# A Gram block of 64 tokens by 133 split into two of 32 by 95, four side by side in the array's columns, and the blocks of the first image set apart from each other

## The chip, the cores and the metric

The kernel runs on one core of a Trainium2 chip. The metric is the device time of the program in microseconds. Three runs of the kernel before gave 2585.49, 2586.68 and 2586.95 us; their median, 2586.68 us, is the time before. The profile shown is of a further execution.

## The reference, cut to what matters

Eight images of 768 channels and 32 x 32 tokens go through two layers. The first is a group norm and an attention with 12 heads, whose scores come from the variances of keys and values, then a projection and the residual. The second layer is what the change is about:

```python
norm = jnp.sqrt(jnp.sum(feature * feature, axis=1, keepdims=True))
feat_n = feature / jnp.maximum(norm, EPS)
feat_pad = jnp.pad(feat_n, ((0, 0), (0, 0), (PAD, PAD), (PAD, PAD)))
corr = jnp.stack([jnp.sum(feat_pad[:, :, r:h + r, cc:w + cc] * feat_n, axis=1) for r, cc in _offsets()], axis=1)
x = jnp.concatenate([feature, corr], axis=1)
out = jnp.einsum('bchw,oc->bohw', x, conv_w) + conv_b[None, :, None, None]
```

`feature` is the group norm of the first layer's result. The 28 offsets lie within three rows and three columns of a token. So `corr` needs, for each token, dot products over the 768 channels with some of its neighbours.

## The kernel before, in words

**The Gram blocks.** By symmetry only neighbours in the same row and in the three rows below are computed. Each image is cut into 8 blocks of 4 rows by 32 columns (`t` from 0 to 7), and each block into a left and a right half of 16 columns. `Corr.gram(t)` (from L1140) computes the products of each half's 64 tokens with a window of 7 rows by 19 columns, 133 tokens, around it; the last block has only 4 rows below its top, so 76 tokens. The 64 tokens are the stationary operand and the window is the moving one. The two halves stand side by side in the array's columns: the left half writes partitions 0 to 63 of the PSUM tile `gr`, the right half 64 to 127. There are 6 chunks of 128 channels, so a gram has 12 matmuls in the program. All is fp32, and the hardware runs each fp32 matmul as two, so the trace has 24 per gram.

**Around it.** `Corr.turn(t)` (L1138) puts the stationary tokens of block t into one contiguous tile `turn`: two instructions, one per half. They run on POOL for images 0 to 6, where `turnpool` has one buffer, so block t+1 is turned when gram t has read the tile; for the last image they run on ACT, into buffers of the pool `expool`. After the matmuls, `out` copies the PSUM tile to one of the tiles `win` (by DVE; by ACT for the last image), of which two alternate for t from 0 to 6, and SyncE stores it to DRAM (`windowed`, L1171): two DMAs of 64 rows. After the grams 3 and 7 the diagonals are read back (`dd`, L1185), scaled with the inverse norms (`rn` by POOL at L1201, `dn` by DVE), transposed by TensorE (`ct`, L353), stored (L1222), gathered (L1233 to L1239) and multiplied to `cs`, the 28 correlation channels. The matmuls of L1059, L1272 and L1370 add them to the convolution. They have 28 rows of the array by 128 columns.

**Other widths of matmul.** Nearly all other matmuls go in halves of 64 columns too: `halves` (L350) for keys, values, projection and convolution, and L800 for the attention's products (`av`). `ones_products` (L831, tile `den`) is the one place that uses four groups of 32 columns: four matmuls of 32 x 512 in the program, eight in the trace.

**What sets the order.** The order on every engine is fixed when the program is built. A planner (`Clock`) holds a time of its own; every unit of TensorE work has a planned duration (`KV_US` 1.93, `T_US` 2.58, `STEP_US` 1.73, `GRAM_US` 1.4), and jobs for other engines are put in at planned times (`later.after`). In the loop over b, image b's attention runs next to the second layer of image b-1. `work_off` alternates: an attention run of four steps (16 matmuls `av` in the program) when its exponentials are planned to be there, otherwise the next unit of `rest`. The grams of image b-1 lie in the list `beside`; `next_to` takes the first of them. It is called before and after every attention run, and from places inserted in `rest` (at 3 and 7; in the turn b = 1, which has the first image's grams, at 7, 11 and 15). `remaining` takes what is left near the end of `rest`. The last image's eight grams stand in `rest` in a row, after two units.

**Who reads what.** In `rest` at (d = 1, n = 0) a unit also emits `make_sums` (L636 to L642), eight POOL instructions for the tile `s`. POOL does them in the order in which they are emitted, among the turns.

Of the kernel before, what the change touches and what calls it, by code (L numbers as in the profile page):

```python
# [13 lines left out]
P = 128  # L14
NB, C, H, W = 8, 768, 32, 32
N = H * W
J = C // P
NH, HD = 12, 64
HP = NH // 2
MT = N // P  # L20
# [7 lines left out]
RUNS = ((0, 0, 4), (31, -1, 3), (62, -2, 5), (93, -3, 7))  # L28
HW = W // 2
TALL, WIDE = MT // 2 + 3, HW + 3  # L30
AHEAD_OF = [o for first, _, count in RUNS for o in range(first, first + count)][1:]
NA = len(AHEAD_OF)
PAD = 99
SPAN = TALL * WIDE
WIN = SPAN + 3
PITCH = WIN + 3
# [17 lines left out]
TAIL = 0.0  # L54
EXP, SUM, STEP_US = 1.07, 1.15, 1.73
KV_US, T_US, CORR_US = 1.93, 2.58, 1.2
GRAM_US = 1.4
WARM, BRIDGE = 42, (3, 7)


# [13 lines left out]
FOUR = P // 4  # L74
# [12 lines left out]
def windows(ap, *dims):  # L87

    return bass.AP(tensor=ap.tensor, offset=ap.offset, ap=[list(d) for d in dims])


class Clock:


    def __init__(self):
        self.now, self.count, self.jobs = 0.0, 0, []
        self.act, self.rows, self.poll = 0.0, ([], []), lambda: None
        self.dve = 0.0

    def after(self, us, job):  # L100
        self.count += 1
# [71 lines left out]
def two_layers(ctx, tc, x, wkv, wproj, bproj, wconv, wcorr, bconv, out):  # L173
# [28 lines left out]
    clock = Clock()  # L202
    later = clock
    vector = Vector(nc.vector, clock)
    ready = set()
# [4 lines left out]
    def other(shape, name):  # L210
        return smp.tile(shape, F32, tag="sm", name=name)
# [16 lines left out]
    def act_copy(us, to, at):  # L228
        nc.scalar.copy(to, at)  # L229
        clock.act = max(clock.act, clock.now) + us  # L230
# [172 lines left out]
    for j in range(J):  # L403
        for hf, queue in enumerate((nc.sync, nc.scalar)):
            at = slice(hf * HF, (hf + 1) * HF)
# [18 lines left out]
    for base, sign in ((0, 1), (3, -1)):  # L424
        nc.gpsimd.affine_select(
            out=group, in_=group, compare_op=ALU.is_ge, fill=0.0, base=base,
# [25 lines left out]
    windowed = [dconst.tile([MT, P * (PITCH + 2)], F32, name=f"windowed{i}") for i in range(2)]  # L452
# [668 lines left out]
    class Corr:  # L1121
# [18 lines left out]
        def gram(self, t):  # L1140

            b = self.b
            tall = min(TALL, H - 4 * t)
            n = tall * WIDE
            if t not in self.turned:
                self.turn(t)
            block = self.turned[t]
            ps = other([P, SPAN], f"gr{b}_{t}")
            for j in range(J):
                image = self.f[:, j, :].rearrange("p (y x) -> p y x", x=W)  # L1150
                for side in range(2):
                    left = side * (HW - 3)
                    nc.tensor.matmul(  # L1153
                        ps[side * HD : (side + 1) * HD, :n].rearrange("p (y x) -> p y x", x=WIDE),
                        lhsT=block[:, j, side, :],
                        rhs=image[:, 4 * t : 4 * t + tall, left : left + WIDE],
                        start=j == 0, stop=j == J - 1,
                    )
            for ahead in range(t + 1, min(t + (3 if b == NB - 1 else 2), MT)):
                if ahead not in self.turned:  # L1160
                    self.turn(ahead)

            def out():
                win = wins[t % 2 if t < MT - 1 else 2]
                if b < NB - 1:
                    vector.tensor_copy(win[:, :n], ps[:, :n])
                else:
                    act_copy(0.3, win[:, :n], ps[:, :n])
                for side in range(2):
                    to = windowed[b % 2][t : t + 1, side * (HD * PITCH + HD - 3) :]  # L1170
                    nc.sync.dma_start(  # L1171
                        out=windows(to, (HW * PITCH - 3, 4), (PITCH, HW), (1, WIN)), in_=win[side * HD : (side + 1) * HD, :]
                    )
                if t % 4 == 3:
                    later.after(4.0, lambda: self.diagonals(t // 4))

            later.after(GRAM_US + 0.25, out)

        def diagonals(self, hf):
# [48 lines left out]
        def gather(self):  # L1228
# [6 lines left out]
            for n, (first, apart) in enumerate(PICKED):  # L1235
                k, row = 3 * n, 2 + AHEAD_OF.index(first)
                nc.sync.dma_start(out=u[k : k + 3, :], in_=windows(r[row : row + 1, PAD:], (apart * ROW, 3), (1, N)))
# [15 lines left out]
    class Conv:  # L1253
# [24 lines left out]
        def low_residual(self):  # L1278
            self.early = True
            for n in range(JH):  # L1280
                later.after(1.5 * n, lambda n=n: self.residual(n))
# [106 lines left out]

    def remaining(beside):
        while beside:  # L1390
            next_to(beside)

    def next_to(beside):

        if beside and ready.issuperset(beside[0][1]):
            us, _, unit = beside.pop(0)
            unit()
            clock.pass_time(us)
# [94 lines left out]
    def next_image(b):  # L1493
        load_image(b)
        xn = images[b]
        clock.after(12.0, lambda: first_norm(b, xn, 1.2, lambda norm: norm.apply(xn, xn, ("xn", b), 1.2)))
# [34 lines left out]
    def fill_t(count):  # L1531
        for n in range(count):
            later.after(1.0 * n, t_stream.fill)

    def start_corr(b):
        corrs.append(Corr(b, layer1[b][0]))
        corrs[-1].turn(0)

    second, corrs = [], []
# [5 lines left out]
    for b in range(NB + 1):  # L1545
        rest, attention, ots, beside = [], None, None, []
        if b < NB:

            ots = [v.rearrange("p t r d -> p (t r d)") for v in kv.vt]
            rest += kv.units(1)  # L1550
            if b:
                rest.insert(len(rest) - 5, (0.0, (), lambda: conv.low_residual()))
            attention = Attention(b, kv, ots)
        if b:
            has_f = ("f", b - 1),
            if b > 1:
                clock.wait(*has_f, ready=ready)
            f, acc = layer1[b - 1] if b > 1 else first_f * 2
            corr = corrs.pop() if 1 < b < NB else Corr(b - 1, f) if b == NB else None
            conv = Conv(  # L1560
                b - 1, f, images[b] if b < NB else acc, (lambda b=b: next_image(b + 1)) if b + 1 < NB else lambda: None
            )
            if b < NB:

                def low_residual(b=b, f=f):
                    for n in range(JH):
                        later.after(1.5 * n, lambda n=n: nc.sync.dma_start(out=f[:, n, :], in_=xv[b, :, n, :]))

                conv.then = low_residual
            grams = [(GRAM_US if t < MT - 1 else 0.9, has_f if b > 1 else has_f + ("turned",), lambda t=t: (corr or corrs[0]).gram(t)) for t in range(MT)]  # L1570
            first, start = (0.0, has_f, conv.sums.first), (0.0, (), conv.start)
            if b < NB:
                beside = grams
                for n in (3, 7) if b > 1 else (7, 11, 15):
                    rest.insert(n, (0.0, has_f, lambda: next_to(beside)))
                rest.insert(len(rest) - 4, (0.0, has_f, lambda: remaining(beside)))
                rest.insert(len(rest) - 4, first)
                rest += [start] + conv.units()
                if b == NB - 1:
                    rest.insert(len(rest) - 3, (0.0, (), conv.set_aside))  # L1580
            else:
                units, parts = conv.units(), conv.corr_units()
                rest += [first, start] + units[:2] + grams + units[2:17]
                for n, unit in enumerate(units[17:]):
                    rest += parts[n : n + 1] + [unit]
        else:
            more = [(us, (("xn", 1),) * (n > 1), unit) for n, (us, _, unit) in enumerate(kv1.units(0))]
            rest.insert(len(rest) - 3, (0.0, (), lambda: apply_second(0)))
            rest += [(0.0, (), lambda: apply_second(1))] + more[:20] + [(0.0, (), lambda: fill_t(3))] + more[20:]
            rest += [(0.0, (), lambda: fill_t(TBLOCKS - 3))]  # L1590
        work_off(rest, attention, beside)
        assert not beside
        if b < NB:
            project(b, ots, conv.wide if b == NB - 1 else None)
            if b == 0:
                kv = kv1
                kv.place_values()
            elif b + 1 < NB:
                clock.wait(("xn", b + 1), ready=ready)
                kv = KeysValues(b + 1, images[b + 1])  # L1600
                units = kv.units(0)
                units.insert(len(units) - 6, (0.0, (("f", b),), lambda: start_corr(b)))
                work_off(units)
            else:
                clock.wait(("f", b), ready=ready)
# [36 lines left out]
```

## Time and profile before

| | |
|---|---|
| median of three runs | 2586.68 us |
| the profiled execution, its own time | 2586.23 us |
| its span, first to last instruction | 2584.4 us |
| TensorE matmuls `gr` of 64 x 133 and 64 x 76 in the trace | 1344 and 192 |
| TensorE's clock | 1.0 over the whole span |
| DMA | 448.18 MB, mean 173 GB/s |
| SyncE: stores of `windowed` | 128, each 503 to 711 ns of issue (median 518) |

Some words on reading. A matmul's duration in the trace includes the time until its last result is out, and matmuls overlap, so a stream is read from the distance of the starts. The view by groups gives the busy time of a group with overlaps counted once. In the timeline the columns are the start (us), the length (us), engine, line, operation, result and operands, rows x columns of the array, shape and number; in brackets stands the engine's idle time before it and what ended it. PEld is the loading of the stationary operand. Some matmul records can be missing.

### The profile page before, as it was taken

How to read it: one execution, taken by the hardware profiler on the slowest of the kernel's cores; microseconds unless marked ns; L12 is line 12 of the kernel's file. 1: busy time of each engine (PE TensorE's matmuls, PEld its weight loads, DVE VectorE, ACT ScalarE, POOL GpSimd, SP SyncE). 2: the span in 40 equal slices, each digit the busy share in tenths (PEclk: the TensorE clock that was granted, in tenths of full speed). 3: DMA queues.
4: the chain of work that ended last, by engine and by line, in shares of the span. 5: the costliest groups of instructions: out<-in, count | busy, mean ns of one | idle time of the engine just before them, and what ended most of it. 6: DMA issues, size and time to landing. Idle time of an engine off the chain costs nothing.

```text
span 2584.4 us, 40568 instructions
## 1 busy us (share of the span) xinstructions
PE 2577.0 (100%) x14798; PEld 1317.4 (51%) x14798; DVE 1614.2 (62%) x4117; ACT 1367.6 (53%) x1844; POOL 426.0 (16%) x449
## 2 busy tenths in 40 slices
PE   9999999999999999999999999999999999999999
PEld 5654364444764347643456434664347443575333
DVE  6868835775347853478534885358853578536874
ACT  1497179801697117970179701897018970199600
POOL 4320130004300043000430004300033001331000
PEclk9999999999999999999999999999999999999999
DMA  8866366355563655636556365563655636545333
GB/s 294 290 224 222 102 210 187 119 195 170 184 202 102 198 168 175 206 97 208 167 174 201 97 212 171 169 199 108 216 171 159 208 109 215 164 142 166 116 111 108
DMA packets 324718, 448.18 MB, mean 173 GB/s; under 512 B 59811, under 2 KB 245523, under 8 KB 324519
## 3 DMA queue, kind: packets, MB, share of 16 engines
q1 hardware_dynamic: 322454, 442.24, 53.6%
q10 hardware_dynamic: 2064, 3.34, 0.4%
q8 instruction: 118, 1.93, 0.3%
q14 instruction: 82, 0.66, 0.1%
HBM read 376.70 MB, written 64.40 MB: 171 GB/s over the span
## 4 chain that ended last, share of the span: by engine, by line
PE 98%; POOL 1%; DVE 0%; issue 0%; DMA 0%; ACT 0%; SPq 0%; POOLq 0%; ACTq 0%; DVEq 0%
PE x L350 35%; PE av L800 25%; PE y L350 18%; PE z L350 10%; PE own L350 5%; PE gr L1153 3%; PE den L831 1%; PE warm L419 1%; PE den L887 1%; POOL turn L1138 0%; PE y L1059 0%; PE z L1059 0%; PE cc L1272 0%; DVE acc L167 0%; DMA windowed<-win 0%
## 5 line engine op out<-in xcount | busy, mean ns | idle before, releaser
L774 ACT ACTIVATE ex<-bc,nk 128x1024 f32<-128x1024 f32 x768 | 827.3, 1137 | 414.3 <-DVE v L167 146.5
L800 PE MATMUL av<-ex,v 128*64 128x512 f32 x3072 | 692.1, 593 | 0.1
L800 PEld LDWEIGHTS av<-ex,v 128*64 128x64 f32 x3072 | 325.2, 137 | 323.0 <-issue 209.9
L784 ACT ACTIVATE junk<-bk,vm 128x1024 bf16<-128x1024 f32 x368 | 420.4, 1142 | 28.4 <-DMA bk<-kdr 18.8
L167 DVE TENSOR_TENSOR acc<-acc,ex 128x1024 f32<-128x1024 f32 x300 | 344.6, 1211 | 0.0
L229 ACT COPY kp<-x 128x384 f32<-128x384 f32 x28 | 13.3, 478 | 510.1 <-PE x L350 508.6
L350 PE MATMUL y<-kv,s 128*64 128x384 f32 x1488 | 265.7, 487 | 0.4 <-POOL s L636 0.4
L350 PE MATMUL x<-kv,xn 128*64 128x384 f32 x1512 | 259.9, 486 | 0.0
L350 PE MATMUL x<-kv,s 128*64 128x384 f32 x1488 | 257.3, 487 | 0.0
L350 PEld LDWEIGHTS x<-kv,xn 128*64 128x64 f32 x1512 | 136.6, 137 | 107.0 <-issue 85.9
L350 PEld LDWEIGHTS x<-kv,s 128*64 128x64 f32 x1488 | 140.0, 137 | 93.9 <-issue 72.7
L350 PEld LDWEIGHTS y<-kv,s 128*64 128x64 f32 x1488 | 134.3, 137 | 94.2 <-issue 76.0
L530 POOL TENSOR_TENSOR rstda<-vea,neghalf 128x1 f32<-128x1 f32 x8 | 4.8, 595 | 965.1 <-DVE vea L167 965.1
L1138 POOL TENSOR_TENSOR turn<-f,ones 128x384 f32<-128x384 f32 x112 | 110.9, 1010 | 242.7 <-PE gr L1153 167.9
L350 PE MATMUL z<-kv,xn 128*64 128x384 f32 x768 | 133.5, 486 | 0.0
L350 PE MATMUL x<-f,wt 128*64 128x512 f32 x504 | 118.3, 592 | 0.0
L167 DVE TENSOR_TENSOR v<-y,v 128x128 f32<-128x128 f32 x180 | 40.9, 282 | 117.9 <-PE y L350 117.9
L636 POOL TENSOR_TENSOR s<-xn 128x384 f32<-128x384 f32 x64 | 65.7, 1035 | 281.9 <-PE x L350 169.4
L167 DVE BATCH_NORM_STATS2 vbn<-v 128x6 f32<-128x64 f32 x720 | 101.5, 209 | 0.0
L350 PEld LDWEIGHTS z<-kv,xn 128*64 128x64 f32 x768 | 72.4, 137 | 49.8 <-issue 40.3
L1153 PEld LDWEIGHTS gr<-f,turn 128*64 128x64 f32 x1344 | 87.0, 136 | 14.3 <-issue 6.1
L167 DVE SCALAR_TENSOR_TENSOR xn<-x,bconv_sb,xn 128x512 f32<-128x512 f32 x63 | 46.3, 745 | 76.5 <-PE x L350 75.3
(206 smaller groups left out, 3144.9 us busy)
## 6 DMA issues: line engine op xcount, KB each, us to landing
kv<-kvs SPq DMA_DIRECT2D x124, 576.0 KB
kv<-in_wkv_dram SPq DMA_DIRECT2D x95, 576.0 KB
bc<-vdr SPq DMA_DIRECT2D x96, 512.0 KB
f<-in_x_dram SPq DMA_DIRECT2D x48, 512.0 KB
bk<-kdr SPq DMA_DIRECT2D x46, 512.0 KB
x1d<-f SPq DMA_DIRECT2D x42, 512.0 KB
xn<-x1d SPq DMA_DIRECT2D x42, 512.0 KB
out_dram<-xn SPq DMA_DIRECT2D x82, 256.0 KB
```

The source lines that it names most:

```text
L167: return getattr(self.engine, name)(*args, **kw)
L229: nc.scalar.copy(to, at)
L350: nc.tensor.matmul(out[at], lhsT=lhsT[:, at], rhs=rhs, start=start, stop=stop, **kw)
L419: nc.tensor.matmul(warm[:, 0:P], lhsT=ident, rhs=ident, start=True, stop=True)
L636: nc.gpsimd.tensor_tensor(self.sums[g][:, 0], a[g][2], a[g][3], ALU.add)
L774: nc.scalar.activation(ex, self.bc[e], AF.Exp, scale=self.kv.nk[self.half][:, h, t : t + 1])
L784: nc.scalar.activation(junk, self.bk[e], AF.Exp, scale=self.kv.m2[self.half][:, h, t : t + 1], accum_out=self.sums[:, e, t : t + 1],)
L800: nc.tensor.matmul(self.av[hf][e * HD : (e + 1) * HD, :], lhsT=self.vt[:, t, e, :], rhs=exs[e][:, hf * HF : (hf + 1) * HF], start=t == 0, ...
L831: nc.tensor.matmul(den[at * 32 : (at + 1) * 32, :], lhsT=ones[:, 0:32], rhs=self.acc[e][:, hf * HF : (hf + 1) * HF], start=True, stop=True,)
L887: nc.tensor.matmul(den[e * HD : (e + 1) * HD, :], lhsT=ones, rhs=self.acc[e][:, at], start=True, stop=True)
L1138: nc.gpsimd.tensor_tensor(to[:, :, side], half, windows(ones, ones.ap[0], (0, J), (HW, 4), (1, HW)), ALU.mult)
L1153: nc.tensor.matmul(ps[side * HD : (side + 1) * HD, :n].rearrange("p (y x) -> p y x", x=WIDE), lhsT=block[:, j, side, :], rhs=image[:, 4 * ...
```

## The change

The group of stationary tokens becomes 32 (2 rows by 16 columns), so a block has four of them: left and right half, upper and lower two rows. Each group needs only 5 rows of window: 5 x 19 = 95 tokens. The four groups write partitions 0, 32, 64 and 96 of the same PSUM tile. A gram has 24 matmuls of 32 x 95 in the program in place of 12 of 64 x 133. The last block keeps its 76 tokens, now also in four groups. Each store of a half becomes two stores of 32 rows, with the lower one two rows further down, except for the last block.

For the order: the planner counts 1.08 us for a gram instead of 1.4 (0.87 for the last block instead of 0.9), and `next_to` gives out no gram until 1.08 + 2.3 us of planned time have passed since the one before began (`remaining` ignores this). In the turn b = 1 the places in `rest` are 7 and every second one from 12 to 28.

```diff
-GRAM_US = 1.4
+GRAM_US, TURN_US = 1.08, 2.3
...
-            tall = min(TALL, H - 4 * t)
+            last, tall = t == MT - 1, min(SHORT, H - 4 * t)
...
+            clock.turned = clock.now + GRAM_US + TURN_US
...
-                for side in range(2):
-                    left = side * (HW - 3)
+                for at in range(4):
+                    side, low = at // 2, at % 2
+                    left, first = side * (HW - 3), 4 * t + (0 if last else 2 * low)
                     nc.tensor.matmul(
-                        ps[side * HD : (side + 1) * HD, :n].rearrange("p (y x) -> p y x", x=WIDE),
-                        lhsT=block[:, j, side, :],
-                        rhs=image[:, 4 * t : 4 * t + tall, left : left + WIDE],
+                        ps[at * FOUR : (at + 1) * FOUR, :n].rearrange("p (y x) -> p y x", x=WIDE),
+                        lhsT=block[:, j, side, low * FOUR : (low + 1) * FOUR],
+                        rhs=image[:, first : first + tall, left : left + WIDE],
                         start=j == 0, stop=j == J - 1,
                     )
...
-                for side in range(2):
-                    to = windowed[b % 2][t : t + 1, side * (HD * PITCH + HD - 3) :]
+                size, count, down = (WIN, 4, 0) if last else (SHORT * WIDE + 3, 2, 2 * (HW * PITCH - 3 + WIDE))
+                for first in range(0, P, count * HW):
+                    side, low = divmod(first, HD)
+                    to = windowed[b % 2][t : t + 1, side * (HD * PITCH + HD - 3) + (down if low else 0) :]
                     nc.sync.dma_start(
-                        out=windows(to, (HW * PITCH - 3, 4), (PITCH, HW), (1, WIN)), in_=win[side * HD : (side + 1) * HD, :]
+                        out=windows(to, (HW * PITCH - 3, count), (PITCH, HW), (1, size)),
+                        in_=win[first : first + count * HW, :size],
                     )
...
     def remaining(beside):
         while beside:
+            clock.turned = 0.0
             next_to(beside)
...
-        if beside and ready.issuperset(beside[0][1]):
+        if beside and ready.issuperset(beside[0][1]) and clock.now >= clock.turned:
...
-                for n in (3, 7) if b > 1 else (7, 11, 15):
+                for n in (3, 7) if b > 1 else (7,) + tuple(range(12, 30, 2)):
                     rest.insert(n, (0.0, has_f, lambda: next_to(beside)))
```

More of the change, by code (lines that the diff above doesn't have):

```diff
@@ L30 @@
 TALL, WIDE = MT // 2 + 3, HW + 3
+SHORT = 2 + 3
 AHEAD_OF = [o for first, _, count in RUNS for o in range(first, first + count)][1:]
@@ L97, in __init__ @@
         self.act, self.rows, self.poll = 0.0, ([], []), lambda: None
-        self.dve = 0.0
+        self.dve = self.turned = 0.0
     def after(self, us, job):
@@ L1569, in two_layers @@
                 conv.then = low_residual
-            grams = [(GRAM_US if t < MT - 1 else 0.9, has_f if b > 1 else has_f + ("turned",), lambda t=t: (corr or corrs[0]).gram(t)) for t in range(MT)]
+            grams = [(GRAM_US if t < MT - 1 else 0.87, has_f if b > 1 else has_f + ("turned",), lambda t=t: (corr or corrs[0]).gram(t)) for t in range(MT)]
             first, start = (0.0, has_f, conv.sums.first), (0.0, (), conv.start)
```

## The prediction

> **What bounds the kernel.** The page first: its span, the busy times, and the chain that ended last.
>
> ```profile
> span 2584.4 us, 40568 instructions
> ...
> PE 2577.0 (100%) x14798; PEld 1317.4 (51%) x14798; DVE 1614.2 (62%) x4117; ACT 1367.6 (53%) x1844; POOL 426.0 (16%) x449
> ...
> PE 98%; POOL 1%; DVE 0%; issue 0%; DMA 0%; ACT 0%; SPq 0%; POOLq 0%; ACTq 0%; DVEq 0%
> ```
>
> TensorE is never without work and makes 98% of the chain. So a change is worth what it takes from TensorE's stream of columns, less the stalls it adds; a shorter copy of `win` is worth nothing. The groups by shape give the durations for single matmuls, but these overlap, so I read the timeline of TensorE, where the distance of the starts is the price. First two grams of 133 columns with an attention run between, then a last gram of 76.
>
> ```profile
> 1307.17 2.12 PE L350 MATMUL y<-kv,s 128*64 128x384 f32 x12
> 1309.11 1.54 PE L1153 MATMUL gr<-f,turn 128*64 128x133 f32 x24
> 1310.46 7.05 PE L800 MATMUL av<-ex,v 128*64 128x512 f32 x32
> 1317.33 1.54 PE L1153 MATMUL gr<-f,turn 128*64 128x133 f32 x24
> 1318.69 0.51 PE L350 MATMUL x<-kv,xn 128*64 128x384 f32 x2
> ```
>
> ```profile
> 1352.20 0.97 PE L1153 MATMUL gr<-f,turn 128*64 128x76 f32 x24
> 1352.99 2.44 PE L350 MATMUL x<-kv,s 128*64 128x384 f32 x14
> ```
>
> A gram of 133 takes 1318.69 - 1317.33 = 1.36 us, twelve rounds of two matmuls side by side, 113 ns a round; a gram of 76 takes 0.79 us, 66 ns a round. 32 `av` take 6.87 us: 16 rounds of 429 ns. All lie on one line, 0.833 ns per column and 2.5 ns. Entering and leaving a gram costs nothing: all neighbours are 64 columns wide.
>
> Then the one place that already runs four groups of 32 columns, the denominators, by matmuls (first three rows) and by weight loads.
>
> ```profile
> 2423.45 1.46 PE L350 MATMUL y<-f,wt 128*64 128x512 f32 x6
> 2424.84 1.06 PE L831 MATMUL den<-acc,ones 128*32 128x512 f32 x8
> 2425.84 1.94 PE L800 MATMUL av<-ex,v 128*64 128x512 f32 x8
> ```
>
> ```profile
> 2424.84 0.16 PEld L831 LDWEIGHTS den<-acc,ones 128*32 128x32 f32 x8 [0.81 <-DVE v L167]
> 2425.84 0.20 PEld L800 LDWEIGHTS av<-ex,v 128*64 128x64 f32 x4 [0.84 <-issue]
> 2426.32 0.14 PEld L800 LDWEIGHTS av<-ex,v 128*64 128x64 f32 x2 [0.29 <-issue]
> ```
>
> Two things are seen. Four groups do run at once: eight matmuls of 512 columns take two rounds. And the change of width costs time: the last `y` round starts at 2423.45 + 2 x 0.43 = 2424.31, the second `av` round at 2426.32. Four rounds lie between (one y, two den, one av), 4 x 0.429 = 1.72 us, but 2.01 us passed: **0.29 us** for going to 32 columns and back. It consists of about 0.10 without a stream on either side, and first weight loads that nothing hides. The other `den` groups show the same distances.
>
> **The grams in the stream.** A round of 95 columns is 0.833 x 95 + 2.5 = 82 ns; four groups at once make twelve rounds, 0.98 us. The order of the changed program shows each of the 56 grams of the first seven images alone between matmuls of 64 columns, so each pays the change of width: 0.98 + 0.29 = 1.27 us instead of 1.36. 49 grams x -0.094 = -4.6 us. The seven last blocks keep 76 columns, so twelve rounds of 66 ns stay and only the change of width is added: 7 x 0.286 = +2.0 us. Together -2.6 us. With no price for the width it would be 49 x 0.38 = -18.6 us. The Trainium skill bears on this: "TensorEngine Tiling (Array Packing)", Key Properties, says that a change of tiling mode drains TensorE, without a figure; its Theoretical Speedup (2x up to 64 columns, 4x up to 32) would give the -18.6. I take the row, which has both.
>
> **Dispatch.** 48 matmuls and 48 loads per gram, 10 ns per instruction, is denser than any long stretch of the trace: a gram of 76 has 48 instructions in 0.79 us, 16.5 ns each. Here a rule speaks against the change: "TensorE: Matmul & The Clock Gate", Wait — 56ns, not 53.3ns?, says that starts are never under about 25 ns apart. By it a gram is 48 x 25 = 1.20 us plus 0.29: 49 x (+0.13) + 7 x (+0.70) = +11.3 us. The row says otherwise for groups side by side: a single `den` matmul is at least 592 ns long, so the eighth starts no later than 1.06 - 0.59 = 0.47 us after the first, and the second round cannot start before 512 x 0.833 = 0.43; the four of a round are within 0.04 us. The eight loads take 0.16 us together. So I take no floor, with the bounds 0 and, if 16.5 ns per instruction were a limit (131 ns a round), 49 x 0.50 + 7 x 1.08 = +32 us.
>
> **The order in the first image.** Timeline of TensorE there:
>
> ```profile
> 355.64 1.46 PE L1153 MATMUL gr<-f,turn 128*64 128x133 f32 x21 [0.26 <-POOL turn L1138]
> ...
> 359.39 1.46 PE L1153 MATMUL gr<-f,turn 128*64 128x133 f32 x21 [0.23 <-POOL turn L1138]
> ...
> 388.32 0.40 PE L353 MATMUL it<-ident,invs 128*64 128x128 f32 x2 [0.15 <-DVE invs L167]
> 389.10 0.44 PE L353 MATMUL ct<-ident,dn 128*64 128x128 f32 x4 [0.37 <-DVE ir L167]
> ```
>
> The brackets count from the end of the last result; from the end of the stream the holes are 0.47, 0.45, 0.32 and 0.54 us (for the first: a gram matmul started at 354.94 and `y` at 354.90 with 0.32 of columns, so it streamed until 355.22; the gram came at 355.64, and its second load added 0.05). Two turns take 1.99 us after a gram, and only one unit of 1.93 us stood between. In the changed order two units or a whole attention run stand between any two grams there, and a unit now stands between `it` and `ct`. POOL's eight sums (7.9 us) now come ahead of turn 5; from the row times they end about when the attention run before gram 5 does, so up to 0.3 us may come back. I take -1.6 us, between -1.8 and -0.5.
>
> **The other six images.** There gram 4 comes after five units instead of three, the sums of POOL ahead of turn 5, and gram 7 some 3.9 us later. Turn 5 has an attention run (6.87 us) as cover. `cs` was stored until 758.9 us for its use at 781.56, so 3.9 us later costs nothing. Gram 1 comes close behind its turn (gram 980.79, turn done 980.41): a gram 0 shorter by 0.09 can make it wait by that much: +0.3 us in all, at most 0.6.
>
> **Stores.** 112 more DMAs go through SyncE, ahead of loads of weights and rows queued there. A store of 64 rows takes 518 ns of issue, one of 20 rows (L1222) 323, so one of 32 rows some 380: a gram's stores take 1.5 us instead of 1.0. SyncE spends longer than that waiting (108 us for `win` alone), and TensorE never waited for a DMA load; I count 0. Without that cover it is 0.5 us per gram, 28 us.
>
> **The last image.** Its eight grams stand in a row, so they pay one change of width, but they don't run at TensorE's pace now: 2516.12 to 2527.43, 11.3 us, where 7 x 1.36 + 0.79 = 10.3. Waits between 2513 and 2530 us:
>
> ```profile
> ACT win L229 <- DMA windowed<-win: 2.0, 3, 1.5
> ```
>
> A `win` tile is free when its stores have landed, about 3.1 us after the copy, and two alternate: 1.57 us a gram. Four stores make this longer by up to 0.5 us per pair of grams. The first grams gain some 0.4 us each until the tiles bind. I take +0.4 with the change of width, between -0.9 and +1.5.
>
> **The sum.** -4.6 + 2.0 - 1.6 + 0.3 + 0.4 = -3.5 us. The profiled execution took 2586.23 (span 2584.4 and 1.8 around it), 0.45 under the median of the three runs; it would be 2582.7, and the median **2583.2 us**. About 0.2%, 5.2 us, is what a measurement can tell from no change, so this is within it.
>
> **The rivals.**
> - *Dispatch limits the four groups* (18%), the slower end. The place is the 672 rounds of the 56 grams; the sum turns at 3.5 / 672 = 5 ns more a round, 87 ns or 10.9 ns per instruction. At 25 ns a matmul it is +11.3 - 1.6 + 0.3 + 0.4 = +10.4, **2597 us**; at the outer bound 2618. For it: nothing so dense for so long is in the trace. Against: the four `den` starts.
> - *New waits from the order* (20%): TensorE has almost no holes before, so a reordering of POOL, SyncE and the copies can only open some. 0.5 to 1 us in each of seven images gives 2587 to **2590 us**.
> - *The change of width is cheaper than at `den`* (12%), where the loads and the following instructions might be late for reasons of their own. At half the price, 56 x 0.14 = -8 more: **2575 us**; at nothing, 2567. Against: 17 `den` groups between different neighbours agree.
> - The forecast's own case has 50%: 2580 to 2586.5.
>
> Faster than 2581.5: the cheap width and a quarter of the own case, 0.25. Slower than 2591.9: dispatch and a quarter of the waits, 0.23. Range 2578 to 2595: leaves out the cheapest widths and the worst of dispatch.
>
> **What would show it.** In the profile after: grams of 95 whose neighbours' starts lie 1.27 us apart more than their own columns, with holes of 0.10 us on either side; rounds of 82 ns inside (if 100: dispatch); grams of 76 at 1.08 us in all; no TensorE wait for `turn` in the first image; the last image's eight still near 11.3 us. It is wrong if rounds are over 87 ns, if the holes at the edges are missing, or if TensorE waits for `s`, `turn`, `kv` or `wt` where it did not.

## The result, and the profile after

The changed kernel takes **2589.26 us**, the median of 22 runs (2587.94 to 2592.14), beside 2586.61 for the kernel before in as many runs. The ratio is 1.0012 with a 95% interval of 1.0006 to 1.0017. It is slower, by some 2.65 us (0.1%), where the forecast had 3.5 us faster. The profiled execution took 2588.0 us, 1.8 more than that of before.

The page of the kernel after: span, busy times, chain.

```profile
span 2586.3 us, 43803 instructions
...
PE 2574.5 (100%) x16334; PEld 1217.4 (47%) x16334; DVE 1610.0 (62%) x4117; ACT 1367.1 (53%) x1844; POOL 427.1 (17%) x449
...
PE 97%; DMA 1%; DVE 1%; ACT 0%; SPq 0%; issue 0%; POOLq 0%; POOL 0%; ACTq 0%; DVEq 0%
```

TensorE is still 97% of the chain, where it was 98%: there are now waits in it. The timeline of TensorE shows whether the grams themselves are as forecast. A gram between `y` and an attention run, the next gram behind that run, and a last block of 76 columns:

```profile
1304.10 2.11 PE L351 MATMUL y<-kv,s 128*64 128x384 f32 x12
1306.13 1.19 PE L1156 MATMUL gr<-f,turn 128*32 128x95 f32 x48
1307.25 7.09 PE L801 MATMUL av<-ex,v 128*64 128x512 f32 x32
1314.27 1.19 PE L1156 MATMUL gr<-f,turn 128*32 128x95 f32 x48
...
1352.64 1.00 PE L1156 MATMUL gr<-f,turn 128*32 128x76 f32 x48
1353.57 2.16 PE L351 MATMUL y<-kv,s 128*64 128x384 f32 x12
```

From gram to `av` it is 1.12 us, 0.98 of rounds and 0.14 for leaving the width. From `av` to the next gram it is 7.02 us, 6.87 of `av` and 0.15 for entering. So a gram of 95 costs 1.27 us, as forecast (the gram of 76 gives way to `y` 0.93 us behind its start, 0.79 + 0.14); no dispatch limit shows. In the first image, at the places of the stalls (the second gram, `it`, `ct`), the same view has:

```profile
357.12 1.19 PE L1156 MATMUL gr<-f,turn 128*32 128x95 f32 x48
...
390.33 0.32 PE L354 MATMUL it<-ident,invs 128*64 128x128 f32 x1
...
392.33 0.48 PE L354 MATMUL ct<-ident,dn 128*64 128x128 f32 x3
```

No bracket with a releaser stands behind them: TensorE waits for nothing there.

Where is the time then? I took the same matmul in both traces, at points where both have done the same work except for the form of the grams:

| TensorE reaches | before, us | after, us | difference |
|---|---|---|---|
| the first `av` ahead of the first image's grams | 343.12 | 342.68 | -0.44 |
| the `av` behind that image's second layer | 504.92 | 502.77 | -2.15 |
| the same one image later | 809.09 | 806.58 | -2.51 |
| the same, five images behind the first | 2085.57 | 2081.33 | -4.24 |
| the last image's first gram | 2516.12 | 2513.10 | -3.02 |
| `y` behind the last image's eighth gram | 2527.37 | 2528.33 | +0.96 |
| the `cc` matmuls near the end | 2566.53 | 2568.39 | +1.86 |

So the kernel gains until 2085 us, loses 1.6 us before the last image's grams (1.2 in the table, because the seventh image's grams gain another 0.4 on the way), **4.0 us in those eight grams**, and 0.9 behind them. First the grams; the timeline of TensorE, before and then after, with the `y` that follows them:

```profile
2516.12 7.08 PE L1153 MATMUL gr<-f_last,turn 128*64 128x133 f32 x120
...
2527.37 3.17 PE L350 MATMUL y<-t1f,wt 128*64 128x512 f32 x14
```

```profile
2513.10 3.15 PE L1156 MATMUL gr<-f_last,turn 128*32 128x95 f32 x144
...
2519.88 1.67 PE L1156 MATMUL gr<-f_last,turn 128*32 128x95 f32 x48 [2.18 <-ACT win L230]
2522.37 2.13 PE L1156 MATMUL gr<-f_last,turn 128*32 128x95 f32 x48 [0.82 <-ACT win L230]
...
2527.41 1.00 PE L1156 MATMUL gr<-f_last,turn 128*32 128x76 f32 x48 [0.32 <-ACT win L230]
2528.33 1.94 PE L351 MATMUL y<-t1f,wt 128*64 128x512 f32 x8
```

From the fifth gram (2519.88) on they come 2.5 us apart: 2522.37, and 2527.41 two further on. TensorE waits for the copy to `win`, and the waits of the same stretch say for what the copy waits (before: 2.0 us, 3 times):

```profile
ACT win L230 <- DMA windowed<-win: 9.8, 5, 2.4
PEld gr L1156 <- ACT win L230: 5.5, 5, 2.4
```

SyncE's queue gives the pace. Its row for the stores, first in the kernel before, then after:

```profile
2517.99 9.58 SPq L1171 DMA_DIRECT2D windowed<-win  x12
```

```profile
2515.42 17.74 SPq L1176 DMA_DIRECT2D windowed<-win  x28
```

Before, twelve stores of mostly 512 ns fill 6.3 of 9.6 us; SyncE waits for TensorE. After, 28 stores follow each other without a wait: each takes 567 to 576 ns (the first two longer), with 44 ns to the next or, between two grams, 103. That is 0.63 us a store and 2.5 us a gram. SyncE has become the engine that limits this stage; the experiments test this.

TensorE's clock halves in the same stretch. This is the window from 2520.7 to 2527.1 us; the last three columns are TensorE's granted clock, the DMA share and GB/s:

```profile
2520.70:2527.10 6.40, 5.10 (x120) 4.08 (x111) 0.00 (x0) 1.30 (x4) 0.00 (x0) 0.50 0.09 23
```

Hence the gram that took 2.13 us. Whether this is a cause or a consequence is a question for the experiments.

The other two losses. In the last attention the kernel before has two units of convolution between two runs of `av`; after, 64 `av` follow each other. TensorE, before and then after, and the waits of after from 2430 to 2446 us:

```profile
2425.84 7.09 PE L800 MATMUL av<-ex,v 128*64 128x512 f32 x32
2432.76 2.74 PE L350 MATMUL x<-f,wt 128*64 128x512 f32 x12
...
2437.91 7.04 PE L800 MATMUL av<-ex,v 128*64 128x512 f32 x32
```

```profile
2430.17 15.03 PE L801 MATMUL av<-ex,v 128*64 128x512 f32 x63
```

```profile
PEld av L801 <- ACT ex L775: 2.7, 5, 0.9
```

31 rounds of 429 ns are 13.3 us; from the first `av` to the last (2445.04) it is 14.9. So 1.6 us went into waiting for exponentials, which in the old order are made while the units run. And the second transposes of `dn` now have a wait ahead of them, 0.79 us from the end of the stream; before, they had none (the row of before, then that of after):

```profile
2543.04 0.39 PE L353 MATMUL ct<-ident,dn 128*64 128x128 f32 x4
```

```profile
2544.85 0.44 PE L354 MATMUL ct<-ident,dn 128*64 128x128 f32 x4 [0.63 <-DVE dn L168]
```

### The profile page after: what moved, and what is told of

Its sections match the earlier page's. It is cut to its first block, busy times and chain, and to the rows that moved or that the text cites. A ratio compares the mean times of both kernels' runs of the same rounds, so it can differ in the third digit from the quotient of the medians.

```text
span 2586.3 us, 43803 instructions
## 1 busy us (share of the span) xinstructions
PE 2574.5 (100%) x16334; PEld 1217.4 (47%) x16334; DVE 1610.0 (62%) x4117; ACT 1367.1 (53%) x1844; POOL 427.1 (17%) x449
## 3 DMA queue, kind: packets, MB, share of 16 engines
q8 instruction: 130, 2.13, 0.3%
## 4 chain that ended last, share of the span: by engine, by line
PE 97%; DMA 1%; DVE 1%; ACT 0%; SPq 0%; issue 0%; POOLq 0%; POOL 0%; ACTq 0%; DVEq 0%
PE x L351 35%; PE av L801 25%; PE y L351 17%; PE z L351 10%; PE own L351 5%; PE gr L1156 2%; PE den L832 1%; PE den L888 1%; DMA xn<-in_x_dram 0%; DMA bc<-vdr 0%; ACT ex L775 0%; PE y L1060 0%; PE z L1060 0%; PE cc L1278 0%; SPq L1176 0%
## 5 line engine op out<-in xcount | busy, mean ns | idle before, releaser
L801 PEld LDWEIGHTS av<-ex,v 128*64 128x64 f32 x3072 | 298.2, 137 | 345.8 <-issue 255.8
L351 PEld LDWEIGHTS x<-kv,s 128*64 128x64 f32 x1488 | 131.4, 137 | 102.6 <-issue 89.9
L351 PEld LDWEIGHTS x<-kv,xn 128*64 128x64 f32 x1512 | 120.8, 137 | 120.3 <-issue 109.0
L351 PEld LDWEIGHTS y<-kv,s 128*64 128x64 f32 x1488 | 115.9, 137 | 114.1 <-issue 102.1
L351 PEld LDWEIGHTS z<-kv,xn 128*64 128x64 f32 x768 | 66.4, 137 | 57.7 <-issue 53.2
L351 PE MATMUL x<-v,wt 128*64 128x512 f32 x384 | 91.6, 592 | 0.0
L351 PEld LDWEIGHTS x<-f,wt 128*64 128x64 f32 x504 | 61.4, 137 | 44.6 <-issue 27.2
```

The source lines that it names most:

```text
L351: nc.tensor.matmul(out[at], lhsT=lhsT[:, at], rhs=rhs, start=start, stop=stop, **kw)
L801: nc.tensor.matmul(self.av[hf][e * HD : (e + 1) * HD, :], lhsT=self.vt[:, t, e, :], rhs=exs[e][:, hf * HF : (hf + 1) * HF], start=t == 0, ...
```

## The experiments

Every kernel was timed 10 to 21 times beside the kernel before (e16, further below, only once). Differences are in us against the median of before, timed beside it. Four groups were timed together: e1 to e4; e5, e6, e8, e9; e7, e10, e11, e12; e13, e14, e15. Between groups a difference of 1 us is not resolved: e10 and e15 are the same kernel and differ by that much.

| kernel | median | ratio, 95% interval | difference |
|---|---|---|---|
| e1_last_image_wide | 2585.03 | 0.9995 (0.9987 to 1.0003) | -1.2 |
| e2_only_last_narrow | 2589.89 | 1.0014 (1.0007 to 1.0020) | +3.7 |
| e14_four_stores | 2589.27 | 1.0013 (1.0006 to 1.0019) | +3.2 |
| e3_win_tiles | 2587.80 | 1.0004 (0.9996 to 1.0013) | +1.6 |
| e4_pool_queue | 2586.73 | 1.0002 (0.9994 to 1.0011) | +0.5 |
| e8_warm | 2591.67 | 1.0023 (1.0014 to 1.0032) | +5.5 |
| e6_order_only | 2586.01 | 1.0001 (0.9993 to 1.0010) | -0.1 |
| e7_no_order | 2587.71 | 1.0007 (0.9999 to 1.0015) | +1.3 |
| e12_old_plan | 2588.71 | 1.0010 (1.0004 to 1.0017) | +2.3 |
| e11_wide_upper_store | 2590.24 | 1.0015 (1.0008 to 1.0023) | +3.8 |
| e9_last_plan | 2583.61 | 0.9989 (0.9983 to 0.9996) | -2.5 |
| e5_best | 2581.57 | 0.9982 (0.9976 to 0.9989) | -4.6 |
| e10_best_old_plan | 2580.62 | 0.9980 (0.9971 to 0.9989) | -5.8 |
| e13_old_order_narrow7 | 2581.23 | 0.9981 (0.9973 to 0.9988) | -4.9 |
| e15_new_order_narrow7 | 2581.33 | 0.9981 (0.9974 to 0.9989) | -4.8 |

Theory A: the number of stores on SyncE makes the last image's loss. Its rivals: B, the loss lies in the first seven images; C, too few tiles `win`; D, the halved clock; G, the 32-wide matmuls.

### Is it the last image? (e1, e2)

e1 is the changed kernel with the old form for the last image:

```diff
-            last, tall = t == MT - 1, min(SHORT, H - 4 * t)
+            last, narrow = t == MT - 1, self.b < NB - 1
+            tall = min(SHORT if narrow else TALL, H - 4 * t)
...
-                for at in range(4):
-                    side, low = at // 2, at % 2
+                for at in range(4 if narrow else 2):
+                    side, low, m = (at // 2, at % 2, FOUR) if narrow else (at, 0, HD)
...
```

> The changed kernel, but the last image's eight grams keep the form of before: two groups of 64 x 133 and two stores each. Theory A (SyncE: the last image's 28 narrow stores take 0.62 us each of SyncE's time, one after another, 2.5 us a gram, and both TensorE's grams and the read-back behind the stores wait for that): the first seven images keep the 3.0 us by which TensorE was ahead at the last image's first gram, and the last image costs what it cost before, so 2583.6 us, 0.9988 of before. Rival B (something spread over the first seven images was lost that the trace of one execution hides): stays at 2588 to 2589.

e2 has `narrow = self.b == NB - 1`, in the order of before.

> The kernel before with its old order, only the last image's eight grams in four groups of 32 and with their four stores. Theory A: +3.9 us in the row of grams, +0.8 where the transposes of dn come too early for their data, +0.1 for the change of width: 2591.4 us, 1.0019 of before. Rival B: within 1 us of before.

The row of grams in e1, then in e2:

```profile
2512.64 7.08 PE L1157 MATMUL gr<-f_last,turn 128*64 128x133 f32 x120
...
2523.89 5.32 PE L351 MATMUL y<-t1f,wt 128*64 128x512 f32 x24
```

```profile
2515.78 3.15 PE L1156 MATMUL gr<-f_last,turn 128*32 128x95 f32 x144
...
2530.92 5.92 PE L351 MATMUL y<-t1f,wt 128*64 128x512 f32 x24
```

With the old form the row takes 11.25 us as before, with the new one 15.1. e2 alone loses 3.7 us; e1 ends 1.2 us under before (its interval includes no change), 3.8 us better than the changed kernel. So B falls: the last image is the place. But both missed: e1 was expected at 2583.6 and came to 2585.03, e2 at 2591.4 and came to 2589.89. The trace of e1 still has the wait ahead of the second `dn` transposes (0.79 us) that I had counted to the stores, and the 64 `av`; e2 has neither. So these two are not SyncE's. e1 and e2 differ there in the new order with its planned durations.

### The stores, the tiles, the clock (e14, e3, e4, e8)

e14 is the kernel before, with only the last image's stores cut in two:

```diff
-                for side in range(2):
+                count = 2 if b == NB - 1 and t < MT - 1 else 4
+                for first in range(0, P, count * HW):
+                    side, low = divmod(first, HD)
```

> The kernel before in everything but the last image's stores: its first seven grams keep two groups of 64 x 133, and each half is stored in two stores of 32 rows by 136 elements instead of one of 64. Theory A (number of stores on SyncE): 28 stores at 0.62 us, 17.4 us in a row, the row of grams 15 us instead of 11.3, TensorE waits 1 us or more behind most grams: +3.7 us as with the narrow grams, 2590 us, ratio 1.0014. Rival G (the groups of 32, with their denser matmuls, have a part in the row's length): less than +2 us.

It loses 3.2 us (interval 1.6 to 4.9) with matmuls of 64 x 133 in the row. TensorE's timeline:

```profile
2516.20 5.72 PE L1153 MATMUL gr<-f_last,turn 128*64 128x133 f32 x96
2522.64 1.58 PE L1153 MATMUL gr<-f_last,turn 128*64 128x133 f32 x24 [0.71 <-ACT win L229]
2525.16 1.58 PE L1153 MATMUL gr<-f_last,turn 128*64 128x133 f32 x24 [0.95 <-ACT win L229]
...
2531.05 2.32 PE L350 MATMUL y<-t1f,wt 128*64 128x512 f32 x10
```

The same 2.52 us from gram to gram, and 14.85 us for the row. The clock, by windows of the same trace:

```profile
2522.70:2530.90 8.20, 5.37 (x92) 4.62 (x94) 0.62 (x2) 2.34 (x7) 0.00 (x0) 1.00 0.10 28
```

The clock is full throughout. So neither the 32-wide matmuls (G) nor the halved clock (D) is needed for the loss.

e3 gives each of the first seven grams a `win` tile of its own:

```diff
...
-                win = wins[t % 2 if t < MT - 1 else 2]
+                win = wins[2] if last else self.wins[t] if b == NB - 1 else wins[t % 2]
```

> The changed kernel with seven tiles win for the last image's first seven grams instead of two that alternate (five lie in the buffer of the turns, which the last image does not use). No copy waits for a store any more. Theory A (SyncE's issue is the pace): the 28 stores still follow each other at 0.62 us for 17.4 us; the row of grams gets shorter, to 9 to 11 us, but the read-back comes no earlier, so the hole moves to the transposes of dn, from 0.8 to 5 us or more: 2589 us, within 1 us of the changed kernel. Rival C (the number of win tiles is the limit, by the time a store takes to land): the row of grams takes 10 us and nothing is late behind it: 2583 to 2584.

The grams now take 8.7 us and don't wait for stores. But SyncE's row is as long as before, the read-back of `dd` stands behind it, and TensorE waits at the transposes. From SyncE's and TensorE's timelines of e3:

```profile
2520.23 12.50 SPq L1180 DMA_DIRECT2D windowed<-spare  x20
...
2533.43 2.25 SPq L1195 DMA_DIRECT2D dd<-windowed  x4
```

```profile
2538.19 0.69 PE L354 MATMUL ct<-ident,dn 128*64 128x128 f32 x4 [3.05 <-DVE dn L168]
```

The hole moved, as theory A had it (3.2 us from the end of the stream, where 5 or more were expected), and the time is 2587.8, not the 2583 to 2584 of rival C. Some 1.1 us came back, each kernel against before, so the tiles may have a small part.

e4 gives every second of these stores to POOL:

```diff
+                    queue = nc.gpsimd if b == NB - 1 and low else nc.sync
-                    nc.sync.dma_start(
+                    queue.dma_start(
```

> The changed kernel with the lower two rows' stores of the last image's grams (14 of its 30) issued by POOL, which has little to do there, instead of SyncE. Theory A: SyncE's stores fall to 1.24 us a gram, the row of grams takes 10.5 to 12.5 us, the transposes find their data: 2584 to 2586. Rival C (landing time with two win tiles): no gain, 2588.5 to 2590. Rival D (the halved clock of TensorE after its first long wait makes the loss, not the wait)[...].

Measured 2586.73, 2.1 us better than the changed kernel, each against before, and a little short of the expected. Its row of grams takes 13.75 us, where 10.5 to 12.5 were expected, and the second transposes still wait (0.63 us in the brackets). The view of `windowed` of e4 tells what is late next:

```profile
L1177 POOL DMA_DIRECT2D windowed<-win x14: 594/594/937, 2515.5 to 2528.2; - x14
...
  ACT win L230: 6.3, 4
...
DMA to landing us min/median/max: 2.1/2.8/4.3
```

SyncE is no longer full, but POOL's stores land 2.8 us after their issue (in the changed kernel a tile is free some 1.6 to 1.7 us after SyncE has issued its last store), and two tiles then give a gram every 2.1 to 2.2 us. With the queue relieved, rival C is the limit.

e8 keeps TensorE busy with matmuls whose results are not used:

```diff
...
+            if b == NB - 1 and not last:
+                for _ in range(5):
+                    for at in range(4):
+                        rows = slice(at * FOUR, (at + 1) * FOUR)
+                        nc.tensor.matmul(ps[rows, 256:384], lhsT=ident[:, rows], rhs=ident, start=True, stop=True)
```

> The changed kernel with 20 more matmuls of 32 x 128 (5 rounds by four groups, results unused, 1.1 us) behind each of the last image's first seven grams, so that TensorE idles less between them and its clock should not be halved. Theory A (SyncE's stores are the pace, 2.52 us a gram): a gram at half the clock takes 1.9 us and is hidden in the 2.52, so the time stays within 0.7 us of the changed kernel, 2588.5 to 2589.5. Rival D (the halved clock makes the loss): 2.5 to 3.5 us off, 2586.

The clock stayed at 1.0 and nothing was won; it took 2591.67 us, 2.9 us more than the changed kernel, each against before, and outside the expected 2588.5 to 2589.5. SyncE's 28 stores took 17.74 us, to the digit as without these matmuls. The excess has two visible parts: the first copy to `win` waited 1.6 us for the added matmuls, so the stores began later, and there are three holes of 0.55, 0.55 and 1.17 us (from the end of the stream) among the dense matmuls for which the trace names no releaser.

Two kernels of the later sections answer the question without added work. e7 and e12 have the narrow grams and stores of the changed kernel and the planned durations of before, in the old and in the new order. TensorE's clock is 1.0 through the row of e7; in e12 it is 0.5 for 3.4 us, from 2523.8 to 2527.2. From both timelines, e7 first, a gram near the end of the row and the `y` behind it:

```profile
2523.99 1.19 PE L1155 MATMUL gr<-f_last,turn 128*32 128x95 f32 x48 [1.40 <-ACT win L230]
...
2527.38 5.37 PE L351 MATMUL y<-t1f,wt 128*64 128x512 f32 x24
```

```profile
2523.76 2.13 PE L1156 MATMUL gr<-f_last,turn 128*32 128x95 f32 x48 [1.29 <-ACT win L230]
...
2529.73 5.37 PE L351 MATMUL y<-t1f,wt 128*64 128x512 f32 x24
```

The grams of e7 begin at 2512.96, those of e12 at 2515.30, so the rows take 14.42 and 14.43 us. D falls: the slower grams are hidden in the wait for SyncE. The row of the changed kernel is 0.8 us longer (15.23), and by as much its first store starts later: 2.3 us after the first gram, in e7 and e12 1.5, because SyncE was still issuing other transfers.

### What a store costs (e11, e16)

e11 is the changed kernel with full rows in the upper stores of the last image; `wide` takes the place of `size` in both address patterns:

```diff
+                    wide = WIN if b == NB - 1 and not low else size
```

> The changed kernel, but in the last image the stores of the upper 32 rows carry 136 elements a row as before instead of 98 (the further ones are never read); the lower stores stay at 98. It shows what sets SyncE's time for a store. If the number of rows sets it, both kinds take 567 to 576 ns, time as the changed kernel, 2589. If rows under 512 bytes cost more (392 against 544 bytes), the wider ones fall to 300 to 380 ns, a gram's stores from 2.52 to 2.1 us, and the time by about 2 us to 2587.

The view of `windowed` of e11, with minimum, median and maximum in ns:

```profile
L1177 SPq DMA_DIRECT2D windowed<-win x30: 567/570/692, 2518.3 to 2539.7; - x30
```

From the third store on, rows of 136 elements and of 98 both take 567 to 576 ns, and the kernel took 2590.24 us, not the 2587 that cheaper wide rows would have given. The length of a row is not it. e16 is the kernel before with eight stores of 16 rows a gram in the last image:

```diff
+                    for row in range(8):
+                        side, y = divmod(row, 4)
+                        to = windowed[b % 2][t : t + 1, side * (HD * PITCH + HD - 3) + y * (HW * PITCH - 3) :]
+                        nc.sync.dma_start(out=windows(to, (PITCH, HW), (1, WIN)), in_=win[row * HW : (row + 1) * HW, :])
...
```

> The kernel before in all but the last image's stores: each of its first seven grams is stored by eight DMAs, one for each row of 16 tokens (16 x 136 elements, one dimension of rows in the address pattern instead of two). It shows what sets SyncE's time for one store: 64 rows took 503 to 616 ns, 32 rows 567 to 576 at either length of a row, 20 rows in one dimension (rows<-cr) 306 to 330. If the two dimensions of rows cost the time, 16 rows in one dimension take 300 to 340 ns, eight of them 2.7 us a gram; if fewer rows as such take longer, 600 ns or more, 5 us a gram.

```profile
L1173 SPq DMA_DIRECT2D windowed<-win x56: 320/418/1676, 2516.7 to 2546.8; - x56
```

418 ns, between both expectations: 16 rows in one dimension are cheaper than 32 in two, which are dearer than 64 in two (512). So the cost does not fall with the number of rows as I had assumed. The shape does not settle it either: the last block's two stores, 64 rows in every kernel, took 514 and 513 ns in the last image of before and 584 and 568 in that of the changed kernel. What sets the cost stays open. The one run took 2601.79 us beside 2587.96 of before, and its row of grams 21.15 us: the more stores, the longer the row, with the grams unchanged.

### The planned durations (e9, e12, e10)

e9 is e1 with the old planned durations for the last image:

```diff
...
-            grams = [(GRAM_US if t < MT - 1 else 0.87, has_f if b > 1 else has_f + ("turned",), lambda t=t: (corr or corrs[0]).gram(t)) for t in range(MT)]
+            grams = [(((1.4, 0.9) if b == NB else (GRAM_US, 0.87))[t == MT - 1], has_f if b > 1 else has_f + ("turned",), lambda t=t: (corr or corrs[0]).gram(t)) for t in range(MT)]
```

> The changed kernel with the last image's grams in the old form, and with the planned durations of before for them (1.4 and 0.9 us instead of 1.08 and 0.87). The run with the old form alone still had a hole of 0.79 us ahead of the second transposes of dn. Theory E (the shorter planned duration makes the planner put the transposes one unit of 2.6 us closer to each other, and SyncE's stores have no part in that hole): the hole goes, 0.8 us off the run with the old form alone; span 2580.8, median near 2584. Rival: the hole stays and the time with it, because TensorE reaches the transposes 3 us sooner than before.

The wait ahead of `ct` is gone and the median is 2583.61, as expected (its span is 1.1 us longer than expected). e12 sets back all planned durations in the changed kernel:

```diff
-GRAM_US, TURN_US = 1.08, 2.3
+GRAM_US, TURN_US = 1.4, 2.3
...
```

> The changed kernel with one thing set back: the planner counts 1.4 and 0.9 us for a gram, as before, instead of 1.08 and 0.87 (the grams and stores stay narrow). Theory E: the shorter planned durations, not the grams, moved two things. In the last attention, 64 matmuls av follow each other without other work between them and wait for exponentials, 1.3 to 1.6 us; and the second transposes of dn come 2.6 us closer to the first, 0.8 us. Both go: 2589.26 - 2.3 = 2587.0 us; the last row of grams stays at about 15 us. Rival F (those two waits come from TensorE being 4 us earlier there): both stay, 2589.

e10 does the same in the fastest form (with `narrow = self.b < NB - 1 and t < MT - 1`).

> Four groups of 32 only in the first seven blocks of the first seven images; all else in the old form with two stores; the new order, but planned durations of 1.4 and 0.9 us everywhere. Against the fastest so far (2581.57, planned 1.08 in the first seven images) the run of 64 av in the last attention goes: 1.3 to 1.5 us less, 2580.2 us, ratio 0.9977. By rival F no difference from it.

In both traces the 64 `av` and the wait at `ct` are gone: theory E holds for where these waits come from. In time it is less clear. By the differences of the table e9 gained 1.3 us on e1, e10 1.2 on e5, e15, which is the same kernel as e10, only 0.2, and e12 0.4 on the changed kernel, where 2.3 were expected. e12's profiled execution lost 1.15 us at another place, in the first image, where `av` waits for exponentials:

```profile
463.24 2.54 PE L801 MATMUL av<-ex,v 128*64 128x512 f32 x7 [0.98 <-ACT ex L775]
```

### What the order is worth (e6, e7, e13, e15)

e6 is the new order with the old grams and the old planned durations.

> All grams in the old form with two stores, planned durations of before; only the changed order stays (no gram until 2.3 us past the planned end of the one before, more places in the first image). Forecast's terms: -1.6 us in the first image and +0.3 in the six others at most: 2585 us, span 2582.8 to 2583.1. Rival (the order gives nothing, or opens new holes elsewhere): 2586 or more, span 2584 or more.

It comes to 2586.01. e7 is its opposite, the changed grams in the old order (no `turned`, places 7, 11, 15) with the old planned durations.

> The changed grams and stores in all eight images, but the order of before: no pacing, the old places, the old planned durations. Forecast's terms with the corrected one for the last image: -2.6 in the first seven images, +3.9 in the last image's row, +0.15 where TensorE leaves it: 2586.6 + 1.45 = 2588.1 us. If the new order is worth 0.9 us, the kernel with the new order and the old planned durations is 0.9 us below it; by the forecast's 1.6 us, 1.6.

Measured 2587.71, near the expected. e13 and e15 differ in the order alone, with the fastest form of the grams.

> The order, places and planned durations of before; four groups of 32 only in the first seven blocks of the first seven images. 49 x -0.094 = -4.6 us: 2581.8 us, ratio 0.9982, if the order of before loses nothing more with these grams. Beside the same grams with the new order it tells what the order is worth: by the forecast's -1.6 us this kernel is 1.6 us slower than that one, by what the last runs showed (-0.1 and +1.0 us) within 1 us of it.

> The kernel with the new order and planned durations of 1.4 and 0.9 us, grams in groups of 32 only in the first seven blocks of the first seven images, once more, beside the one with the order of before on the same chip. 2580.6 us as before, ratio 0.998.

Three pairs differ in the order alone: before and e6 (-0.1 us with the new order), e7 and e12 (+1.0), e13 and e15 (+0.1). The forecast's -1.6 us is not there.

### The fastest form (e5)

> As the run before it, and the last block of the first seven images (76 columns) in two groups of 64 instead of four of 32, so that no change of width is paid where no columns are saved: 7 x 0.286 = 2.0 us less. Span 2578.8, 5.6 us under before; median 2581 to 2582, ratio 0.998. If the price of the change of width is hidden by something else at these places: no difference from the run before it.

The edit on e9 is `narrow = self.b < NB - 1 and t < MT - 1`. 2581.57 us, as expected: 2.0 us under e9, the price of seven changes of width that saved no columns. e5, e10, e13 and e15 are all faster than both kernels, by 4.6 to 5.8 us than the kernel before, and the simplest, e13, needs nothing of the new order.

## Why the prediction was wrong, step by step

- **The grams in the stream: right.** Five images in a row take the lead from 2.15 to 4.24 us; 0.27 of that is a hole that, of the two executions, only that of before had, so each takes 0.36 us less; forecast 7 x 0.094 - 0.286 = 0.37. Rounds, the price of the width and its two halves are as the `den` rows gave them. The rival of a cheaper width is out. So is that of the dispatch limit: twelve rounds of four matmuls and four loads run in the 0.98 us of their columns, and the Trainium skill's 25 ns between starts ("TensorE: Matmul & The Clock Gate", Wait — 56ns, not 53.3ns?) does not hold for groups side by side here, with four matmuls every 82 ns, 20 ns each.
- **The last image: the step that failed.** "Four stores make this longer by up to 0.5 us per pair of grams ... I take +0.4 with the change of width, between -0.9 and +1.5." It was +4.0, and the sign that the prediction had set itself, eight grams "still near 11.3 us", failed: they took 15.2. I followed the tile (copy, store, landing, 3.1 us for two grams) and added the stores to that loop, but did not ask whether SyncE itself has room. Four stores need 4 x 0.63 = 2.5 us a gram and TensorE, if not held up, takes 1.1 (8.7 us for eight in e3): the queue, not the loop, is the limit. Even with my price of 380 ns and the gaps of 45 between stores it would have been 1.7 us a gram, more than the 1.41 of before, so the mechanism was in reach. The price was wrong besides: it lay between those of 64 rows and of the 20 rows of L1222, another shape, and measured 570 ns. The place is shown by e1 and e2, the stores as the cause by e14, and SyncE's queue, more than the tiles, by e3 and e4.
- **Stores "I count 0": right for the first seven images,** where grams come 5 us or more apart and the leads grow as forecast; there the cover is real. The last image had no such cover, and the sentence had made no exception for it.
- **A step that was missing: the planned durations.** The prediction has no term for the change of GRAM_US and gives no reason for leaving it out. It moves the planner's clock for everything behind the grams: shorter grams let it give out units sooner, so that at the end of the last attention no units were left (1.6 us in the trace) and two transposes came 2.6 us closer (0.8 us). The order is fixed when the program is built, so the row of `av` could have been seen before any run. e9, e10 and e12 show that the waits go with the old numbers; how much time that is worth, 0.2 to 1.3 us, the runs don't settle.
- **The first image's order, -1.6 us: the stalls are gone, the time isn't.** In the kernel after no gram there waits for `turn`, and `it` and `ct` have no hole. But in e7, with the old order, the two waits for `turn` have gone too; whether the change of width gives POOL the time was not tested. Only 0.19 and 0.54 us at `it` and `ct` remain. And TensorE waits at the next thing, `av` for exponentials, at 348 and at 460 us. These holes differ from execution to execution: over the first image the lead changed by between -2.05 and +0.81 us in eleven executions of the new order with narrow grams, by +0.05 and +0.34 in the two of the old order. The hole at 460 us (0.2 to 1.4 us) appears in five of twelve traces of the new order and in none of six of the old; the one at 348 us is in both. That it is the price of the order is argued, not shown; that the sum is near zero is what the three pairs show. The -1.3 us of the one trace below stands close to the forecast's -1.6 by luck.
- **Gram 1 close behind its turn, +0.3:** the leads of the other images, 0.36 us each, show no loss there.
- **The rivals.** The time lies in the band of "new waits from the order" (2587 to 2590), and waits of its kind are there (the 64 `av`, `ct`), 2.4 us in the trace; but they stand at two places near the end, not in each of seven images, and go with the planned durations. The main part, 4.0 us, is none of the three rivals but my own last term, so that the time falls in this band is luck.

By the trace: -2.6 (grams), -1.3 (first image, in this execution), -0.3 (a hole of before), +1.6 (`av`), +4.0 (last image), +0.9 (`ct` and the first `y`): +2.3, which is the table's way from -0.44 to +1.86.

## What to carry to other kernels

When a change splits a transfer, count the issuing engine's own time in each stage against the pace of that stage, not only the way of one buffer; slack over the whole run says nothing about a stage in which the work comes back to back. Where a planner orders the program, a changed duration is a changed order, everywhere behind it: compare the order at the far end too. And a stall removed ahead of another engine's deadline is worth only what that next engine allows.

## What the runs showed of the hardware

- SyncE's time for a store follows neither rows nor bytes: 511 to 520 ns for most of 64 rows (4 x 16; before and e1), 567 to 576 for most of 32 rows (2 x 16) at 98 or 136 elements (the changed kernel, e11), 418 in the median for 16 rows in one dimension (e16). Stores of one shape differ too: those of the last block, 64 rows, took 514 and 513 ns in before and 584 and 568 in the changed kernel.
- TensorE's clock fell to 0.5 from 2520.4 to 2527.3 us in the changed kernel, though its longest wait there was 2.35 us; of the 3.4 us before the fall, from 2517.0 on, it had been busy for 1.24. With waits of 1.1 us in each 2.5 us (e14) it stayed at 1.0. With the same narrow grams 2.5 us apart it stayed at 1.0 in e7 and fell to 0.5 for 3.4 us at 2528.6 in e2. The Trainium skill's "TensorE: Matmul & The Clock Gate", What's actually happening, speaks of an idle window of 3.4 us; here no wait was that long, and a stretch of that length that was mostly idle came before the fall.
